# Rebalancing a five-engine pipeline: bias, norm columns, reciprocal roots and a written order for each of two layers

## The chip, the cores and the metric

One core of a Trainium2 chip runs the whole program. The metric is device time in microseconds, median of the runs. Five engines share the work and each runs its own instructions in order: PE (TensorE; PEld is its weight load), DVE (VectorE), ACT (ScalarE), POOL (GpSimd), and SP (SyncE), which here issues nearly all DMAs. They meet only at semaphores.

## The reference, cut to what matters

The input x is 512 x 512 x 64 in float32. Two equal layers follow each other, `x = x + f(gn(x))`:

- `gn` normalizes 32 groups of two channels over the whole image, so it needs sums over all of x before the first point can be worked on. It is an affine step per channel.
- `xn = ln(gn(x))` over the 64 channels of a point.
- `left`, `right` and `gate` are products of `xn` with 64 x 128 weights, `left` and `right` times a sigmoid of a second product, `gate` a sigmoid.
- A band: `out[i, j] = sum over d in -4..4 of left[i + d, i] * right[i + d, j]`, for each of 128 channels.
- `out = ln(out) * gate` over the 128 channels, then `out @ Wo + bo`, added to x.

## The kernel before

**Tiles and steps.** The rows are cut into 9 blocks (`row_blocks`, line 67), and each block's columns into 2 chunks of 16 steps, 288 steps a layer. A step `t` handles a *unit* of 8 columns from each half of the image, on 128 partitions, as a tile `z` of 128 x (8 x 64) numbers (`load`, line 391). The first layer writes `mid_x`, the second reads it and writes the output; the same generator `layer` (line 739) does both, with `stats` true for the first, which also sums up what the second layer's `gn` needs (`sums`, line 727). Between the layers `mid_stats` (line 924) works out that affine step.

**The path of a unit.** POOL scales and moves it by the group norm (`affine`, line 427; in the first steps of a layer DVE does this). DVE takes statistics (`inner_stats`, line 432, mean and variance of two columns by one instruction). POOL subtracts the mean and multiplies by the reciprocal root (`inner_norm`, line 436). PE transposes it (`transposed`, line 442), ACT copies that out (`kept`, line 461) and it goes to DRAM for later use as well. PE forms two products of four columns each (`right`, line 506), ACT the sigmoid, DVE the product into the ring `RO` (`right_end`, line 513).

**The path of a result.** When a chunk of `RO` is full, PE forms the band with the left factors (`mix`, line 567), two PSUM banks at a time, one copied back into `RO` by ACT and one by DVE. DVE takes the statistics (`out_stats`, line 592), ACT normalizes 8 columns, one instruction each (`norm`, line 631), PE transposes (`turned`, line 668), DVE multiplies by the gate (`times_gate`, line 681), PE multiplies by `Wo` (`end`, line 704), and DVE adds that to the x of that place (`ended`, line 718), which SP has fetched again and to which POOL has added the bias of the layer (`biased`, line 698).

**The roots.** Every four steps `solve` (line 598) turns the variances of four units and four results into reciprocal roots: DVE prepares them with small instructions, and `rsqrt` (line 134) does a first guess on DVE and ten dependent instructions of 128 x 64 on POOL; two more follow there for the results.

**Shifted sums.** Before, the first layer's bias has a per-group mean subtracted, so that the sums it collects are of small numbers, and the second layer's bias has it added again (`shifted`, line 282).

**PSUM.** There are eight banks. `one_bank` (line 128) gives single banks, three in the first layer and four in the second; `two_banks` (line 131) gives pairs, of which there are two. The products, the transposed units and (at the start) the left factors take pairs; gates, turned results, last products and bands take single banks.

**What sets the order.** The loop over `t` (lines 806 to 909) issues everything by wrappers (`en`, line 375) that keep each engine's instructions in the order of the program text, so the order in which the parts stand in that loop is the order in every engine's queue. All of these instructions bear the line of the wrapper, L373, in the profile, and are told apart by their tiles. Tables (`look`, `step`, `count`) place statistics, bands and affine steps in the steps. For POOL the order within a step is: mean and root of the unit after next, scale and move, the roots (every fourth step, one after the other), bias, and then, in those steps, scale and move of one more unit.

Of the kernel before, what the change touches and what calls it, by code (L numbers as in the profile page):

```python
# [30 lines left out]
LN_EPS = 1e-6  # L31

# [47 lines left out]
def tile_two_banded_layers(  # L80
# [35 lines left out]
    nc.vector.memset(all_ones, 1.0)  # L116
    ones_row = const.tile([1, P], F32, name="ones_row")
# [16 lines left out]
    def rsqrt(o: bass.AP, v: bass.AP, vec=nc.vector, e=nc.vector):  # L134


        p, n = v.shape
        t, u = (
            sm.tile([P, 3 * NB], F32, tag=f"rsqrt{i}", name="rsqrt", bufs=1)[:p, :n]
            for i in range(2)  # L140
        )
        vec.tensor_scalar(
            o.bitcast(I32), v.bitcast(I32), -0.5, float(0x5F3759DF), ALU.mult, ALU.add
        )
        e.tensor_tensor(t, o, o, ALU.mult)
        e.tensor_tensor(t, t, v, ALU.mult)
        e.tensor_scalar(u, t, -10.0 / 3.0, None, ALU.add)
        e.tensor_tensor(t, t, u, ALU.mult)
        e.tensor_scalar(t, t, 5.0, None, ALU.add)
        e.tensor_tensor(o, o, t, ALU.mult)  # L150
        e.tensor_tensor(t, o, o, ALU.mult)
        e.tensor_tensor(t, t, v, ALU.mult)
        e.tensor_scalar(t, t, -27.0 / 1024.0, 0.5625, ALU.mult, ALU.add)
        e.tensor_tensor(o, o, t, ALU.mult)


    PARTS = (
        ("right", 2 * H), ("left", 2 * H), ("gate", H), ("Wo", D), ("ob", 1), ("add", 2 * D),
# [60 lines left out]
    def solve_layer(i: int, f: dict, r: dict, tmp, half: bass.AP):  # L219
# [36 lines left out]
        add = r["add"].rearrange("p (t c) -> p t c", c=D)  # L256
        nc.vector.tensor_copy(add[:, 0, :], pb[:, :D])
# [24 lines left out]
    def shifted(i: int, r: dict, tmp):  # L282
        add = r["add"].rearrange("p (t c) -> p t c", c=D)
        if i == 0:

            bias = tmp.tile([P, G], F32, name="bias")
            nc.vector.tensor_reduce(
                bias, add[:, 0, :].rearrange("p (g t) -> p g t", t=2), AX.X, ALU.add
            )
            nc.vector.scalar_tensor_tensor(bias, bias, 0.5, total, ALU.mult, ALU.add)  # L290
            spread(shift, bias)
        op = ALU.add if i else ALU.subtract
        nc.vector.tensor_tensor(add[:, 0, :], add[:, 0, :], shift, op)
        nc.vector.tensor_copy(add[:, 1, :], add[:, 0, :])


# [6 lines left out]
    shift = const.tile([P, D], F32, name="shift")  # L303
# [4 lines left out]
    def group_affine(mean: bass.AP, var: bass.AP, pool):  # L308

        ve = pool.tile([P, D], F32, name="g_ve")  # L310
        nc.vector.tensor_scalar(ve, var, GN_EPS, None, ALU.add)
        rsqrt(ga, ve)
        nc.vector.scalar_tensor_tensor(gb, mean, -1.0, ga, ALU.mult, ALU.mult)
# [113 lines left out]
    def affine(u: Unit, engine):  # L427

        engine.tensor_tensor(u.z, u.z, mid(ga, JU), ALU.mult)
        engine.tensor_tensor(u.z, u.z, mid(gb, JU), ALU.add)  # L430
# [5 lines left out]
    def inner_norm(u: Unit):  # L436
        z = u.z.rearrange("p (k t) c -> p k t c", t=2)
        m = u.mean.unsqueeze(3).broadcast_to([P, JU // 2, 2, D])
        en.gpsimd.tensor_tensor(z, z, m, ALU.subtract)
        en.gpsimd.tensor_tensor(u.z, u.z, last(u.rs, D), ALU.mult)  # L440
# [126 lines left out]
    def mix(c: int, A: bass.AP, h0: int) -> list:  # L567
# [6 lines left out]
        ph = [one_bank().rearrange("i (h t j) -> i h t j", h=q, t=2) for s in range(2)]  # L574
# [23 lines left out]
    def solve(w: dict, ins: list, outs: list, sti, sto):  # L598
# [3 lines left out]
        r = sm.tile([P, 3 * NB], F32, tag="rs", name="rs", bufs=3)[:, : ni + no]  # L602
        if ni:
            en.vector.tensor_scalar(
                v[:, :ni].rearrange("p (k t) -> p k t", t=2), sti[:, : ni // 2, 2::3],
                1.0 / D, LN_EPS, ALU.mult, ALU.add,
            )
            for n, u in enumerate(ins):
                u.rs = r[:, n * JU : (n + 1) * JU]
        if no:  # L610

            js = slice(outs[0].m, outs[0].m + no)
            vo = v[:, ni:]
            en.vector.scalar_tensor_tensor(
                vo.rearrange("p (k t) -> p k t", t=2), sto[:, :, 2::3], 1.0 / H,
                w["m2"][:, js].rearrange("p (k t) -> p k t", t=2), ALU.mult, ALU.mult,
            )
            en.vector.tensor_scalar(vo, vo, LN_EPS, None, ALU.add)
            nm = sm.tile([P, NB], F32, tag="nm", name="nm")[:, :no]
            en.vector.tensor_scalar(  # L620
                nm.rearrange("p (k t) -> p k t", t=2), sto[:, :, 1::3], -1.0, None, ALU.mult
            )
        rsqrt(r, v, en.vector, en.gpsimd)
        if no:
            ro = r[:, ni:]
            en.gpsimd.tensor_tensor(ro, ro, w["m"][:, js], ALU.mult)
            en.gpsimd.tensor_tensor(nm, nm, ro, ALU.mult)
            for n, o in enumerate(outs):
                o.rs, o.nm = ro[:, n * JU : (n + 1) * JU], nm[:, n * JU : (n + 1) * JU]

    def norm(o: Out, lo: int, hi: int):
        if lo == 0:
            o.on = onp.tile([P, JU, H], F32, tag="on", name="on")
        for j in range(lo, hi):
            en.scalar.activation(
                o.on[:, j, :].rearrange("p (h t) -> p h t", t=2), RO[:, :, o.c + j, :],
                AF.Identity, bias=o.nm[:, j : j + 1], scale=o.rs[:, j : j + 1],
            )
# [59 lines left out]
    def biased(o: Out, w: dict, stats: bool):  # L698
        n = S + o.blk.m
        f = o.xr[:n, :, 1 : 1 + 2 * D]  # L700
        add = fewer if stats and o.blk.m < S - WIN else w["add"]
        en.gpsimd.tensor_tensor(f, f, mid(add[:n], JU // 2), ALU.add)

    def end(o: Out, w: dict):
        m = o.blk.m
# [33 lines left out]
    def layer(src: bass.AP, dst: bass.AP, w: dict, stats: bool, then=None):  # L739
# [59 lines left out]
        A, sti, sto, then_affine = {}, {}, None, []  # L799
        for t in range(min(loads), last_t + 3):  # L800
# [21 lines left out]

            mixing, mixed = mixes.get(t, []), []
# [10 lines left out]

# [3 lines left out]
            for v in looking[0:3]:  # L838
                out_stats(*v)
            for u in inputs(t + 2):  # L840
                inner_norm(u)
            if t in units:
                right(units[t], 0, w)
            if t in units:
                right_gate(units[t], 0)
            if t in outs:
                gates(outs[t], w)
            if t in units:
                right(units[t], JQ, w)
            for u in affines.pop(t, []):  # L850
                affine(u, en.vector if u.at < NU + 4 else en.gpsimd)
            if t % 4 == 0 and t > NU:
                then_affine = affines.pop(t + 1, [])
            for v in looking[3:5]:
                out_stats(*v)
            for v in looking[5:]:
                out_stats(*v)
            for v in todo:
                inner_stats(*v)
            if t % 4 == 0:  # L860
                st, us = sti.pop((t + 4) // 4, (None, []))
                so, os = sto or (None, [])
                sto = None
                if us or os:
                    solve(w, us, os, st, so)
            if t in outs:
                gated(outs[t])
            if t in units:
                right_end(units[t], 0)
            if t in outs:  # L870
                biased(outs[t], w, stats)
            if t in outs:
                turned(outs[t], w)
            if t in units:
                right_gate(units[t], JQ)
            for u in inputs(t + 1):
                transposed(u)
            if t in outs:
                times_gate(outs[t], w)
            for u in then_affine:  # L880
                affine(u, en.gpsimd)
            then_affine = []
            if t - 1 in outs:
                end(outs[t - 1], w)
            if t in units:
                right_end(units[t], JQ)
            if len(mixing) > 0:
                c, h0 = mixing[0]
                mixed.append(mix(c, A[c, h0 // HA], h0))
            if t + 1 in outs:  # L890
                norm(outs[t + 1], 0, 4)
            for u in inputs(t + 1):
                kept(u)
            if stats and t - 2 in outs:
                sums(outs[t - 2], t - 2 == first_t, t - 2 == last_t)
            if len(mixing) > 0:
                en.scalar.copy(*mixed[0][0])
            if t - 1 in outs:
                ended(dst, outs[t - 1])
            if t + 1 in outs:  # L900
                norm(outs[t + 1], 4, 8)
            if len(mixing) > 1:
                c, h0 = mixing[1]
                mixed.append(mix(c, A[c, h0 // HA], h0))
            if len(mixing) > 0:
                en.vector.tensor_copy(*mixed[0][1])
            if len(mixing) > 1:
                en.scalar.copy(*mixed[1][0])
            if len(mixing) > 1:
                en.vector.tensor_copy(*mixed[1][1])  # L910
# [136 lines left out]
```

## Time and profile before

| what | value |
|---|---|
| median of 3 runs | 4814.17 us (4813.22 to 4815.75) |
| the profiled execution | 4808.51 us, its span 4806.5 us |
| busy share of the span | PE 79%, DVE 82%, ACT 77%, POOL 79% |
| granted TensorE clock, mean | 0.948 |
| DMA | 983.63 MB moved, 205 GB/s |
| first layer's steady steps | from about 500 to 2400 us |
| second layer's steady steps | from about 2800 to 4600 us |

The shares are taken over the whole span, in which the statistics of the input (the first 250 us) and the change of layers (2400 to 2800 us) use the engines little. What bounds the two long stretches is read from those stretches alone. A row of a group of instructions gives: engine, operation, what it writes and reads, shapes, how many, then busy time, mean duration in ns, and the idle time in front of them with what ended it. A row of the timeline gives start, length, engine, operation and tiles. An instruction's length includes the time in which it has started and doesn't get at its data.

### The profile page before, as it was taken

Reading aid. Unit: us, or ns where it says so; the run is one execution under the profiler, and the core shown is the slowest. Engines: PE = TensorE matmul, PEld = TensorE weight load, DVE = VectorE, ACT = ScalarE, POOL = GpSimd, SP = SyncE. Lnnn points to the kernel's source line nnn. Section 1 sums busy time; section 2 is a strip of 40 time slices with the busy share of each in tenths; the row PEclk is TensorE's granted clock in tenths of the full one; section 3 lists DMA queues with packets and bytes.
Section 4 is the critical chain, followed back from the end, with each engine's and each line's share of the span. In section 5 each row is a group of like instructions: output and inputs, shape, how many; then the busy total and the mean of one; then the engine's idle time right before and its main releaser. Section 6 shows DMA issues by size and latency. Waiting matters only on the chain. (4 is left out here: it accounts for less than half of the span.)

```text
span 4806.5 us, 193543 instructions
## 1 busy us (share of the span) xinstructions
PE 3796.6 (79%) x76306; PEld 3293.0 (69%) x76306; DVE 3929.9 (82%) x9635; ACT 3708.4 (77%) x8732; POOL 3817.1 (79%) x4739
## 2 busy tenths in 40 slices
PE   1025799989999999999985478888888888888888
PEld 0024688878888887888854467777777777777775
DVE  6954788888888888888867478888888888888887
ACT  0013689888888898989883268888888888888899
POOL 0035999999999999999734589999999999999964
PEclk9997999999999999999997689999999999999999
DMA  7859677777777777777763967777777777777876
GB/s 299 336 178 108 172 212 213 215 210 215 211 209 210 211 214 212 214 212 215 199 170 100 105 168 212 216 214 209 217 213 215 213 213 218 210 216 211 222 200 179
DMA packets 1437651, 983.63 MB, mean 205 GB/s; under 512 B 167202, under 2 KB 1284424, under 8 KB 1432392
## 3 DMA queue, kind: packets, MB, share of 16 engines
q1 hardware_dynamic: 1432064, 969.75, 73.6%
q8 instruction: 604, 9.90, 0.9%
q14 instruction: 303, 2.48, 0.2%
q10 hardware_dynamic: 4680, 1.50, 0.1%
HBM read 658.42 MB, written 312.46 MB: 202 GB/s over the span
## 5 line engine op out<-in xcount | busy, mean ns | idle before, releaser
L373 ACT ACTIVATE on<-RO,nm,rs 128x128 f32<-128x128 f32 x4608 | 1927.7, 496 | 15.3 <-PE bank L373 9.9
L373 PEld LDWEIGHTS banks<-pack,zT 64*128 64x128 f32 x18576 | 1251.3, 195 | 549.5 <-ACT zT L373 288.9
L373 PE MATMUL banks<-pack,zT 64*128 64x128 f32 x18576 | 1365.6, 289 | 272.8 <-ACT zT L373 222.6
L373 DVE TENSOR_TENSOR RO<-banks,sg 128x512 f32<-128x512 f32 (+1 forms) x1188 | 795.3, 673 | 228.3 <-POOL sg L373 116.2
L373 DVE SCALAR_TENSOR_TENSOR ZH<-bank,pack,gate 128x448 f32<-128x448 f32 (+1 forms) x1152 | 741.6, 685 | 173.3 <-PE bank L373 97.3
L373 ACT ACTIVATE sg<-banks 128x512 f32<-128x512 f32 (+1 forms) x1188 | 698.0, 589 | 188.6 <-PE banks L373 188.2
L373 DVE BATCH_NORM_STATS2 sto<-RO 128x6 f32<-128x256 f32 x2304 | 800.8, 411 | 3.7
L373 POOL TENSOR_TENSOR z<-z,gb 128x512 f32<-128x512 f32 x536 | 684.8, 1278 | 42.0
L373 PE MATMUL bank<-RO,A 64*64 64x128 f32 x18432 | 706.0, 292 | 3.9 <-ACT RO L373 2.4
L373 PE MATMUL bank<-pack,ZH 128*64 128x64 f32 x18432 | 694.6, 231 | 5.0 <-ACT gate L373 4.1
L373 POOL TENSOR_TENSOR z<-z,ga 128x512 f32<-128x512 f32 x536 | 685.6, 1279 | 3.2 <-DMA z<-mid_x 1.9
L373 POOL TENSOR_TENSOR z<-z,rs 128x512 f32<-128x512 f32 x586 | 619.3, 1057 | 46.0
L373 DVE COPY RO<-bank 128x512 f32<-128x512 f32 x576 | 398.4, 692 | 310.6 <-PE bank L373 307.3
L373 PEld LDWEIGHTS bank<-pack,ZH 128*64 128x64 f32 x18432 | 612.6, 143 | 47.3 <-ACT gate L373 8.5
L373 POOL TENSOR_TENSOR z<-z,sti 128x512 f32<-128x512 f32 x586 | 627.9, 1072 | 0.0
L373 PEld LDWEIGHTS bank<-RO,A 64*64 64x64 f32 x18432 | 582.0, 142 | 43.0 <-ACT RO L373 4.1
L373 ACT ACTIVATE gate<-bank 128x448 f32<-128x448 f32 (+1 forms) x1152 | 565.8, 545 | 34.5 <-PE bank L373 32.0
L373 ACT ACTIVATE zT<-banks 128x512 f32<-128x512 f32 (+1 forms) x1084 | 463.5, 481 | 139.6 <-PE banks L373 128.9
L373 PE MATMUL bank<-zg,pack 64*128 64x448 f32 (+1 forms) x2304 | 564.3, 556 | 4.6 <-DMA zg<-later 4.6
L373 ACT COPY RO<-bank 128x512 f32<-128x512 f32 x576 | 333.2, 579 | 282.3 <-PE bank L373 282.1
L373 PE MATMUL banks<-ident,z 64*128 64x64 f32 x4336 | 254.1, 233 | 359.2 <-DVE RO L373 336.9
L373 DVE BATCH_NORM_STATS2 sti<-z 128x6 f32<-128x128 f32 x2344 | 500.5, 280 | 15.2 <-POOL z L373 14.2
(144 smaller groups left out, 3908.6 us busy)
## 6 DMA issues: line engine op xcount, KB each, us to landing
later<-zT SPq DMA_DIRECT2D x576, 256.0 KB
A<-left_of SPq DMA_DIRECT2D x1152, 128.0 KB
zg<-later SPq DMA_DIRECT2D x576, 256.0 KB
z<-in_x_dram SPq DMA_DIRECT2D x576, 128.0 KB
z<-mid_x SPq DMA_DIRECT2D x576, 128.0 KB
gn_x<-in_x_dram SPq DMA_DIRECT2D x16, 4096.0 KB
XR<-in_x_dram SPq DMA_DIRECT2D x448, 112.0 KB
mid_x<-XR SPq DMA_DIRECT2D x448, 112.0 KB
```

The lines of the kernel that those rows point to most:

```text
L373: return lambda *a, **k: tc.keep_in_program_order(f(*a, **k))
```

## The change

1. **Small forms.** In `solve`, DVE's single-source instructions (`tensor_scalar`) become instructions with two tensors as sources; the epsilon comes from a constant column spread over the width, and a negation is written as `x * 0 - x`. The first guess in `rsqrt` stays as it is.
2. **Norm columns.** Of the 8 columns of a result, ACT normalizes 7 and DVE one (`NV`), by an instruction that reads `RO` and a spread column.
3. **Inner columns.** In the first layer 2 of a unit's 8 columns are centred and scaled by DVE, one instruction a column (`ZV`), and POOL's two instructions cover the other 6; in the second layer nothing moves. The first 17 units are left as they were.
4. **Chains.** `rsqrt` returns its ten POOL instructions as a list, and the loop issues them two at a time between other work; scale and move, and mean and root, are no longer next to each other.
5. **Bias.** The first layer adds both layers' biases (`both`), so that what it stores already holds the second layer's; the second layer issues no bias instruction. `mid_stats` takes that addition out of the sums again, by some small instructions. `shifted` goes.
6. **PSUM.** In the first layer the two banks of a band come as a pair (`APART`), in the second as single banks, as before.
7. **Order.** The loop over the parts of a step follows a list, one for each layer.

```diff
+APART = (False, True)
+ZV = (2, 0)
+NV = (1, 1)
+FIRST = [
+    ("out stats", 2), "centre", "scale", "gates", ("out stats", 3), "inner stats", "bias",
+    "gated", ("project", 0), ("out stats", 99), ("project", 4), "inner columns", "rescale",
+    "turn", "solve", ("sigmoid", 0), ("sigmoid", 4), "last product", ("norm", (0, 4)),
+    "scale next", "move", "move next", ("roots", 2), "sums", ("right", 0), ("roots", 2),
+    ("right", 4), "transpose", "times gate", "keep", ("band", 0), ("band", 1),
+    "norm columns", ("copy a", 0), "end", ("roots", 2), ("copy a", 1), ("copy b", 0),
+    ("roots", 2), ("norm", (4, 8)), ("copy b", 1), ("roots", 99),
+]
+SECOND = [
+    "gates", "scale", "move", ("project", 0), "inner stats", ("project", 4),
+    ("out stats", 2), "centre", ("sigmoid", 0), ("out stats", 3), ("out stats", 99),
+    ("right", 0), "rescale", "inner columns", "gated", "solve", "scale next",
+    ("sigmoid", 4), ("roots", 2), "turn", "last product", "transpose", "times gate",
+    ("band", 0), ("roots", 2), ("norm", (0, 4)), ("roots", 2), "keep", "end", ("right", 4),
+    ("band", 1), ("copy a", 0), "norm columns", ("copy b", 0), ("copy a", 1), ("roots", 2),
+    ("norm", (4, 8)), ("roots", 99), "move next", ("copy b", 1),
+]
...
-    def inner_norm(u: Unit):
-        z = u.z.rearrange("p (k t) c -> p k t c", t=2)
-        m = u.mean.unsqueeze(3).broadcast_to([P, JU // 2, 2, D])
-        en.gpsimd.tensor_tensor(z, z, m, ALU.subtract)
-        en.gpsimd.tensor_tensor(u.z, u.z, last(u.rs, D), ALU.mult)
+    def centred(u: Unit, n: int):
+        m = last(u.mean.rearrange("p k t -> p (k t)")[:, n:], D)
+        en.gpsimd.tensor_tensor(u.z[:, n:], u.z[:, n:], m, ALU.subtract)
+
+    def rescaled(u: Unit, n: int):
+        en.gpsimd.tensor_tensor(u.z[:, n:], u.z[:, n:], last(u.rs[:, n:], D), ALU.mult)
+
+    def inner_columns(u: Unit, n: int):
+        for j in range(n):
+            en.vector.scalar_tensor_tensor(
+                u.z[:, j], u.z[:, j], u.mean[:, j // 2, j % 2 : j % 2 + 1],
+                u.rs[:, j : j + 1].broadcast_to([P, D]), ALU.subtract, ALU.mult,
+            )
...
-        ph = [one_bank().rearrange("i (h t j) -> i h t j", h=q, t=2) for s in range(2)]
+        if APART[0 if stats else 1]:
+            pb = [one_bank() for s in range(2)]
+        else:
+            two = two_banks()
+            pb = [two[:, s * 512 : (s + 1) * 512] for s in range(2)]
...
-            en.vector.tensor_scalar(
-                v[:, :ni].rearrange("p (k t) -> p k t", t=2), sti[:, : ni // 2, 2::3],
-                1.0 / D, LN_EPS, ALU.mult, ALU.add,
+            en.vector.scalar_tensor_tensor(
+                pairs(v[:, :ni]), sti[:, : ni // 2, 2::3], 1.0 / D, eps(ni),
+                ALU.mult, ALU.add,
             )
...
-    def norm(o: Out, lo: int, hi: int):
+    def norm(o: Out, lo: int, hi: int, vector: bool):
...
+            if vector:
+                nm = nm.unsqueeze(2).broadcast_to([P, H // 2, 2])
+                en.vector.scalar_tensor_tensor(to, of, rs, nm, ALU.mult, ALU.add)
+            else:
+                en.scalar.activation(to, of, AF.Identity, bias=nm, scale=rs)
...
-    def biased(o: Out, w: dict, stats: bool):
+    def biased(o: Out, w: dict):
...
-        add = fewer if stats and o.blk.m < S - WIN else w["add"]
+        add = fewer if o.blk.m < S - WIN else both
```

## The prediction

> **What bounds the kernel now.** First the busy time by engine over a long stretch in the middle of each layer, to see whether one engine is full.
>
> ```profile
> 600.00:2200.00 1600.00, 1463.40 (x31066) 1292.29 (x31066) 1372.42 (x3382) 1430.93 (x3332) 1469.33 (x1770) 0.98 0.76 212
> 2800.00:4400.00 1600.00, 1342.77 (x27460) 1178.72 (x27460) 1412.85 (x3396) 1387.89 (x3315) 1480.65 (x1791) 0.95 0.76 211
> ```
>
> After the length the columns are PE, PEld, DVE, ACT and POOL busy, granted clock, DMA share, GB/s. POOL leads in both layers with 92 to 93%, DVE has 86 and 88%. To turn shares into a step I count norm instructions, eight to a step, in the groups of 800 to 2000 us (the first layer):
>
> ```profile
> L373 ACT ACTIVATE on<-RO,nm,rs 128x128 f32<-128x128 f32 x1325 | 555.9, 492 | 1.1 <-ACT sg L373 1.1
> L373 POOL TENSOR_TENSOR z<-z,ga 128x512 f32<-128x512 f32 x168 | 214.9, 1279 | 0.0
> L373 POOL TENSOR_TENSOR z<-z,gb 128x512 f32<-128x512 f32 x168 | 214.8, 1278 | 13.2
> L373 POOL TENSOR_TENSOR z<-z,sti 128x512 f32<-128x512 f32 x166 | 175.3, 1056 | 0.0
> L373 POOL TENSOR_TENSOR z<-z,rs 128x512 f32<-128x512 f32 x165 | 172.1, 1043 | 12.9
> L373 POOL TENSOR_TENSOR XR<-XR,fewer 120x512 f32<-120x512 f32 x166 | 197.3, 1189 | 0.3 <-DMA XR<-in_x_dram 0.2
> ```
>
> 1325/8 = 165.6 steps in 1200 us are 7.25 us a step. The same count in the second layer (1562 norms from 3000 to 4400 us) gives 195.25 steps and 7.17 us. Busy per step is then, first layer: POOL 6.65, PE 6.63, ACT 6.48, DVE 6.21; second: POOL 6.64, DVE 6.33, ACT 6.22, PE 6.02. The rest of POOL's step, about 0.6 us, is idle time in front of its own dependent instructions (the last field of its rows, 98 us in that stretch, 38 of them before the first instruction of the reciprocal roots). So POOL has no time left over; it sets the step.
>
> **What two sources cost on DVE.** The change gives DVE instructions with two tensors in SBUF, beside a busy POOL. The steady stretch has no large one, but the start of each layer has: there DVE scales and moves the units. DVE, then POOL, from 345 us:
>
> ```profile
> 345.93 0.85 DVE L373 TENSOR_TENSOR z<-z,ga 128x512 f32<-128x512 f32 x1
> 346.81 1.41 DVE L373 TENSOR_TENSOR z<-z,gb 128x512 f32<-128x512 f32 x1
> ```
> ```profile
> 346.31 1.37 POOL L373 TENSOR_TENSOR z<-z,rs 128x512 f32<-128x512 f32 x1
> 347.64 1.50 POOL L373 TENSOR_TENSOR z<-z,sti 128x512 f32<-128x512 f32 x1
> ```
>
> and at 303 us on DVE:
>
> ```profile
> 303.44 0.69 DVE L373 TENSOR_TENSOR z<-z,gb 128x512 f32<-128x512 f32 x1
> 304.05 1.54 DVE L373 TENSOR_TENSOR z<-z,ga 128x512 f32<-128x512 f32 x1
> ```
>
> Alone the DVE instruction takes 0.69 us (303.44 in the last fence). At 346.81 it takes 1.41, of which 0.72 is waiting, up to about 0.15 us before POOL's row ends at 347.68. POOL's own rows grow from 1.05 to 1.37 and 1.50. So the two exclude each other for whole instructions. The pair at 304.05 shows the order: two units, independent of each other, and yet POOL gets its turn between them (its row of 303.47 lasts 1.58), so that the second DVE instruction waits for a whole POOL instruction.
>
> **The change part by part.** The profiled execution took 4808.5 us (span 4806.5); the median of the three runs is 4814.2, so 5.7 is added at the end.
>
> *POOL.* In the second layer the bias leaves (1.19 a step: 128x512 group at 1189 to 1190 ns): 6.64 becomes 5.45. In the first, centring and rescaling keep 6 of 8 columns: (1.06 + 1.04)/4 = 0.53 less, 6.12. The interleaved roots and the split of scale and move take away most of the 0.6 us of gaps. POOL no longer bounds: 6.1 to 6.2 and 5.5. What is late next is DVE or PE.
>
> *ACT.* One norm column of eight goes: 0.42 us a step (1.69 for four in a row), leaving 6.06 and 5.80. In steady state it is covered. In the two tails, where a step takes 4.55 us and ACT is 4.24 of it (3.24 for eight norms, 1.00 for the gates), it is not covered: 30 steps a layer x 0.41 x 2 = 24, taken as -20 because the chain's other links remain.
>
> *DVE, own time.* No row shows the new form on 128x64 or 128x128. Between the two-source rows at hand, 186 ns for 128x32 (var<-sto,pack) and 691 for 128x512, a straight line gives 220 and 287 ns; neighbours overlap by some 60 ns (four statistics of 411 ns take 1.40), so 0.15 and 0.22 us each. First layer: 2 x 0.15 + 0.22 = 0.52 a step; second 0.22. So DVE without further waits would be 6.73 and 6.55.
>
> *DVE, waits.* From below, nothing (a form that takes another way to memory); from above, a whole POOL instruction each, 1.28 us. I take the rule of the fences, which are the nearest rows. POOL's five large instructions of the first layer would be 0.79, 0.79, 1.28, 1.28, 1.19; the mean remainder met by chance is the sum of squares over twice the sum, 0.56, less the 0.15 at the end, 0.42; POOL is at work some 85% of the time: 0.36 us for the norm column and for the first inner column. The second inner column follows directly and meets a whole new POOL instruction: mean 1.07 less 0.1, at 80%: 0.75. Together 1.47 us a step in the first layer, 0.36 in the second. Behind the waiting instruction on DVE stand the products `right`, the gate product, the residual sum and the band copies, and PE waits for those to get its PSUM banks back: nothing hides it once DVE is full.
>
> The Trainium skill ("SBUF — State Buffer", section "Who interferes with whom") goes further than these rows: any VectorE instruction with two SBUF inputs contends with a GpSimd instruction that reads SBUF, which takes in the scalar forms used here; by it the sum stays as it is, and without it it is rival A. Its "GPSIMD Engine Reference" (section "Engine selection") speaks for the change: elementwise work belongs on VectorE, twice as fast; by it 0.53 us of POOL would cost DVE 0.30 and the result would again be rival A, but the fenced row of 1.41 us beside POOL is no faster than POOL's 1.28.
>
> *The solve.* Its single-source instructions wait for POOL too (var<-sti has a mean of 501 ns in the first layer's stretch and 665 in the second's, where 0.17 is the least). With two sources they meet the same exclusion; I cost the new forms at 0. If they did not wait, they would give back 0.15 and 0.31 us a step; if each of five met a POOL instruction, that is up to 5 x 1.1/4 = 1.4 us lost, less what it costs now. Against that end: POOL, ahead of DVE, will often be waiting for just this solve.
>
> *Sum.* A full engine still idles a little behind others; I allow 2%. First layer: 1.02 x (6.73 + 1.47) = 8.36, 1.12 more than 7.25, over the 271 steps that have inner columns: +303. Second: 1.02 x (6.55 + 0.36) = 7.05, 0.12 less, x 288: -35. Tails -20. The added dozen small instructions between the layers and the dropped ones of the setup are about 1 us each way. 4808.5 + 303 - 35 - 20 + 5.7 = **5062 us**.
>
> SP's queue keeps its transfers; loads go out in the same place. The new orders move instructions only within a step; I give them no gain, as I see none to read from a row.
>
> **Rivals.** With a factor f on all these waits the sum is -264 + 512 f (first layer 271 x (1.50 f - 0.38), second 288 x (0.37 f - 0.49), tails -20): zero at f = 0.52.
>
> *A, faster:* the scalar form on DVE doesn't queue behind POOL, or POOL mostly stands idle when it comes. At f = 0 the steps are 6.87 and 6.68: 4814 - 264 = 4550; with the solve's waits gone too, some 4430, since PE holds the first layer at 6.63. It decides below a mean wait of about 0.25 us for each such instruction. For it: POOL will have idle time, unlike now, and the fenced rows are of another opcode. Against it: exclusion shows in every pair where both are at work.
>
> *B, slower still:* the bands of the first layer move from the single PSUM banks to the two double ones, which then have four tenants a step instead of three. Now PE waits there already (for DVE's RO 91 us from 800 to 2200). If the late DVE holds both pairs so that PE is late in turn and DVE then waits for PE, I add 0.6 us a step: +163, 5225.
>
> *C, nothing comes of it:* f near 0.5, the second layer's gain pays for the first's loss: 4805 to 4824.
>
> **Chances.** Forecast (4824 to 5200) 0.54, B and beyond 0.17, A 0.26, C 0.03. So faster by over 0.2% 0.26, within 0.2% (about what a measurement of this kernel can tell from no change) 0.03, slower 0.71. The range goes from 4620 (f = 0.14) to 5270 (f = 1.4): about 0.12 lies below it and 0.08 above. The likeliest case's own range is 4824 to 5200.
>
> **What will show it.** DVE's share in the first layer over 95%, POOL's near 75%; the inner-column rows at a mean of 0.5 to 0.9 us instead of 0.22, the norm column at 0.65; POOL's rows of 384 elements longer than 0.79; POOL waiting for the solve longer than now. Rows of 0.22 and 0.29 us beside a busy POOL would make the prediction wrong, and so would a first layer that stays near 7.2 us a step.

## The result and the profile after

The changed kernel takes 5034.4 us (median of 4 runs, 5030.58 to 5046.85), the kernel before 4814.87 beside it: ratio 1.0461 [1.0442, 1.0479]. The forecast was 5062, slower. The profiled execution took 5035.45 us, its span 5033.7, 227.2 more than before.

Where that came from is read from the gate products on DVE, two to a step, in both traces. First product of the first layer: 531.3 us instead of 541.2 (-9.9; over all the runs of this document it lies between 521.9 and 546.9, so this is not read). From first to last product of the first layer: 2279.5 instead of 2015.2 (+264.3). From there to the second layer's first: +1.2. Second layer: 1941.1 instead of 1969.4 (-28.3). What follows: -0.1. As a mean over steps 40 to 250 the first layer goes from 7.23 to 8.30 us a step, the second from 7.14 to 7.07. The whole loss lies in the first layer. Its granted clock is lower too (0.94 instead of 0.98 from 800 to 2200 us), but that is not what costs: executions of the changed kernel with 0.906, 0.934, 0.909 and 0.935 over the span took 5035.45, 5033.36, 5046.85 and 5030.58 us, and the four of e6 below, at 0.925 to 0.950, were fastest at the lowest clock.

Busy time of each engine in a stretch of each layer, changed kernel, columns as in the prediction:

```profile
600.00:2200.00 1600.00, 1337.16 (x26860) 1174.95 (x26860) 1543.41 (x3504) 1178.29 (x2687) 1183.65 (x1536) 0.93 0.66 184
3200.00:4600.00 1400.00, 1242.43 (x24647) 1079.95 (x24647) 1281.95 (x3226) 1188.88 (x2782) 1096.39 (x1392) 0.97 0.78 216
```

In the first layer DVE is busy 96% of the time and POOL 74%: "over 95%" and "near 75%" were forecast. In the second, DVE has 92% and POOL 78%: no engine is full there. The groups of 800 to 2000 us, changed kernel:

```profile
L389 DVE SCALAR_TENSOR_TENSOR z<-z,sti,rs 128x64 f32<-128x64 f32 x290 | 204.9, 746 | 0.0
...
L389 POOL TENSOR_TENSOR XR<-XR,fewer 120x512 f32<-120x512 f32 x145 | 173.7, 1198 | 254.0 <-DMA XR<-in_x_dram 186.8 <-PE banks L389 16.2 <-PE bank L389 13.9
...
L389 POOL TENSOR_TENSOR z<-z,rs 128x384 f32<-128x384 f32 x145 | 121.7, 839 | 0.0
L389 POOL TENSOR_TENSOR z<-z,sti 128x384 f32<-128x384 f32 x144 | 121.0, 840 | 0.0
...
L389 DVE SCALAR_TENSOR_TENSOR on<-RO,rs,nm 128x128 f32<-128x128 f32 x145 | 74.8, 516 | 0.0
...
L389 DVE SCALAR_TENSOR_TENSOR var<-sti,ln_eps 128x32 f32<-128x32 f32 x36 | 28.6, 794 | 0.0
L389 DVE SCALAR_TENSOR_TENSOR var<-sto,pack 128x32 f32<-128x32 f32 x36 | 24.4, 679 | 0.0
```

An inner column takes 746 ns, the norm column 516; POOL's rows of 384 elements take 839 and 840 instead of the 0.79 us that their size would give. The directions were forecast, and the sizes too, but for the norm column (0.65 us). One sign did not come: POOL should have waited longer for the solve, and in the first layer it waits 0.75 us for each instead of 0.83 (31.7 us in 42 solves, 39.8 in 48, 800 to 2200 us); in the second it does, 1.08 instead of 0.50 (3200 to 4600 us). Two things were not forecast. POOL now stands idle for 254 us of 1200 in front of its *bias* instruction, 187 of them for the fetch of `XR`; before, these were 0.3. And the small instructions of the solve wait: the product `var<-sto,pack` took 188 ns before and takes 679.

How an inner column waits, and what POOL waits for, in the timeline of the changed kernel:

```profile
1406.08 0.84 POOL L389 TENSOR_TENSOR z<-z,sti 128x384 f32<-128x384 f32 x1
1406.20 2.04 DVE L389 SCALAR_TENSOR_TENSOR z<-z,sti,rs 128x64 f32<-128x64 f32 x2
...
1406.51 1.03 SPq L389 DMA_DIRECT2D XR<-in_x_dram  x2
...
1406.88 1.28 POOL L389 TENSOR_TENSOR z<-z,ga 128x512 f32<-128x512 f32 x1
...
1410.49 1.20 POOL L389 TENSOR_TENSOR XR<-XR,fewer 120x512 f32<-120x512 f32 x1 [2.33 <-DMA XR<-in_x_dram]
1410.55 1.29 DVE L389 SCALAR_TENSOR_TENSOR on<-RO,rs,nm 128x128 f32<-128x128 f32 x1
...
1416.44 0.46 DVE L389 SCALAR_TENSOR_TENSOR z<-z,sti,rs 128x64 f32<-128x64 f32 x2
```

The pair at 1406.20 takes 2.04 us: its first instruction waits for POOL's of 1406.08, its second until nearly the end of the one of 1406.88 (POOL ends at 1408.16, the pair at 1408.24). The norm column, which starts 0.06 us after a POOL instruction of 1.20, takes 1.29. The pair at 1416.44 meets an idle POOL and takes 0.46. That is the exclusion of the prediction: here DVE and POOL meet not only at semaphores. But POOL had been idle for 2.33 us before 1410.49, and SP had issued that fetch only at 1406.51.

### The profile page after: what moved, and what is told of

Its sections match the earlier page's. It is cut to its first block, busy times and chain, and to the rows that moved or that the text cites. A ratio compares the mean times of both kernels' runs of the same rounds, so it can differ in the third digit from the quotient of the medians.

```text
span 5033.7 us, 192903 instructions
## 1 busy us (share of the span) xinstructions
PE 3947.1 (78%) x76306; PEld 3407.3 (68%) x76306; DVE 4455.6 (89%) x10755; ACT 3532.9 (70%) x8156; POOL 3371.0 (67%) x4451
## 5 line engine op out<-in xcount | busy, mean ns | idle before, releaser
L389 ACT ACTIVATE on<-RO,nm,rs 128x128 f32<-128x128 f32 x4032 | 1705.1, 504 | 23.5 <-POOL nm L389 9.0
L389 PEld LDWEIGHTS banks<-pack,zT 64*128 64x128 f32 x18576 | 1324.7, 203 | 408.0 <-ACT zT L389 232.5
L389 PE MATMUL bank<-zg,pack 64*128 64x448 f32 (+1 forms) x2304 | 741.4, 633 | 170.6 <-DMA zg<-later 111.2
L389 PE MATMUL bank<-pack,ZH 128*64 128x64 f32 x18432 | 667.3, 226 | 3.3 <-ACT gate L389 0.5
L389 POOL TENSOR_TENSOR z<-z,rs 128x512 f32<-128x512 f32 (+1 forms) x586 | 565.0, 965 | 23.3
L389 POOL TENSOR_TENSOR z<-z,sti 128x512 f32<-128x512 f32 (+1 forms) x586 | 568.3, 971 | 0.0
L389 POOL TENSOR_TENSOR XR<-XR,fewer 120x512 f32<-120x512 f32 x224 | 268.5, 1198 | 388.7 <-DMA XR<-in_x_dram 290.1
L389 PE MATMUL bank<-ident,on 64*128 64x64 f32 x9216 | 468.0, 227 | 32.6 <-ACT gate L389 25.7
L389 PEld LDWEIGHTS bank<-ident,on 64*128 64x128 f32 x9216 | 437.7, 141 | 79.2 <-ACT gate L389 33.2
L389 PEld LDWEIGHTS bank<-zg,pack 64*128 64x128 f32 x2304 | 254.3, 197 | 291.4 <-issue 86.2
```

The lines of the kernel that those rows point to most:

```text
L389: return lambda *a, **k: tc.keep_in_program_order(f(*a, **k))
```

## The experiments

The theory was: DVE is full because its two-source instructions wait for POOL (**port waits**). The rivals that the runs weigh: the new order of the first layer, the pair of PSUM banks, the interleaved roots. Steps are means over steps 40 to 250; the DVE share is that of 800 to 2200 us; ratios stand against the kernel before on the same chip. The short names are explained below. Each step time is from one traced execution, on one of several chips, on which the kernel before took medians of 4810 to 4839 us. First layers of the same program differ by 0.03 us a step (e10 and e12), second layers of the same program by up to 0.09 (after, e1, e2, e6 to e9: 7.04 to 7.13). Smaller differences are not read.

| kernel | first layer, us a step | its DVE share | second layer, us a step | ratio to before |
|---|---|---|---|---|
| before | 7.23 | 86% | 7.14 | 1 |
| after | 8.30 | 97% | 7.07 | 1.0461 [1.0442, 1.0479] |
| e1, no inner columns | 8.03 | 90% | 7.13 | 1.0307 [1.0279, 1.0335] |
| e2, inner columns' second source in PSUM | 8.05 | 93% | 7.08 | 1.0305 [1.0286, 1.0323] |
| e3, no columns | 8.05 | 84% | 7.10 | 1.0353 [1.0325, 1.0381] |
| e4, bias alone | 7.19 | 86% | 6.98 | 0.9864 [0.984, 0.9888] |
| e5, e3 with bias last | 7.40 | 87% | 7.14 | 1.0012 [0.9998, 1.0027] |
| e6, after with bias last | 7.73 | 99% | 7.09 | 1.0161 [1.0138, 1.0183] |
| e7, old order with columns | 8.33 | 91% | 7.11 | 1.0465 [1.0432, 1.0497] |
| e8, after with single banks | 8.67 | 92% | 7.04 | 1.0654 [1.0633, 1.0676] |
| e9, e7 with second sources in PSUM | 7.51 | 88% | 7.08 | 1.0023 [1.0014, 1.0033] |
| e10, e4 with the two-source solve | 7.18 | 86% | 6.98 | 0.9848 [0.9831, 0.9864] |
| e11, e4 with interleaved roots | 7.38 | 83% | 7.01 | 0.9963 [0.9948, 0.9978] |
| e12, e10 with a norm column in the second layer | 7.21 | 86% | 6.99 | 0.9871 [0.9854, 0.9887] |

### Taking back the columns, and the bias alone

**e1** puts the inner columns back to POOL:

```diff
-ZV = (2, 0)
+ZV = (0, 0)
```

> The changed kernel with the inner columns given back to GpSimd in the first layer, all else kept (order, norm column, band pair). Port theory (a VectorE instruction with two SBUF sources queues behind GpSimd): VectorE loses 2 x 0.70 us a step of the first layer, which goes from 8.30 to about 7.0 us, 271 steps, so about 4680 us (4640 to 4760). Rival 'work' (VectorE just has more to do, 0.15 us a column): first layer at 8.0, about 4950. Rival 'order' (the new order or the band's pair of banks costs the time): first layer stays above 8, 4950 or more.

**e2** leaves them on DVE, in the same places, but their second source is a block of ones in PSUM. It leaves the reciprocal root out of these columns.

```diff
-                u.rs[:, j : j + 1].broadcast_to([P, D]), ALU.subtract, ALU.mult,
+                ones_ps, ALU.subtract, ALU.mult,
...
+    ones_ps = acc_bank[:, 256 : 256 + D]
+    nc.vector.memset(ones_ps, 1.0)
```

> The changed kernel, but the two inner columns read their second source from a constant tile of ones in PSUM instead of the roots in SBUF; this leaves the multiplication by the root out of those two columns. Count, size and place of the instructions stay. Port theory: their mean goes from 746 to about 220 ns, the first layer to about 7.0 us a step, about 4670 us (4620 to 4760). Rivals 'work' and 'order': nothing changes, 5034 us.

**e3** takes back the norm columns too:

```diff
-ZV = (2, 0)
-NV = (1, 1)
+ZV = (0, 0)
+NV = (0, 0)
```

> The changed kernel without inner columns and without norm columns on VectorE in both layers; order, forms, bias and the band's pair stay. Port theory: another 0.45 us off VectorE and 0.42 us onto ScalarE a step; the first layer near 6.9, the second from 7.07 to about 6.75, in all about 4570 us (4500 to 4680). Rival 'order': the first layer stays above 8 us, the second at 7.05, 4950 or more.

**e4** keeps only part 5 of the change, the bias stored by the first layer; order, small forms, chains and banks are those of before.

```diff
-APART = (False, True)
+APART = (True, True)
-ZV = (2, 0)
-NV = (1, 1)
+ZV = (0, 0)
+NV = (0, 0)
-ORDERS = (FIRST, SECOND)
+ORIG = [
+    ("out stats", 3), "centre", "rescale", ("project", 0), ("sigmoid", 0), "gates",
+    ("project", 4), "scale", "move", ("out stats", 2), ("out stats", 99), "inner stats", "solve",
+    ("roots", 99), "gated", ("right", 0), "bias", "turn", ("sigmoid", 4), "transpose",
+    "times gate", "scale next", "move next", "last product", ("right", 4), ("band", 0),
+    ("norm", (0, 4)), "keep", "sums", ("copy a", 0), "end", ("norm", (4, 8)), "norm columns",
+    ("band", 1), ("copy b", 0), ("copy a", 1), ("copy b", 1),
+]
+SECOND_ORIG = [x for x in ORIG if x not in ("bias", "sums")]
+ORDERS = (ORIG, SECOND_ORIG)
...
-            en.vector.scalar_tensor_tensor(
-                pairs(v[:, :ni]), sti[:, : ni // 2, 2::3], 1.0 / D, eps(ni),
-                ALU.mult, ALU.add,
-            )
+            en.vector.tensor_scalar(
+                pairs(v[:, :ni]), sti[:, : ni // 2, 2::3], 1.0 / D, LN_EPS, ALU.mult, ALU.add
+            )
...
```

> The kernel before with one part of the change alone: the first layer stores the second's bias, and GpSimd has no bias instruction in the second layer. Order, small forms, band banks, all columns as before. Theory: the first layer stays at 7.23; in the second GpSimd falls to about 6.0 us a step with its gaps and VectorE, 6.33 us busy, bounds: 6.5 to 6.7 us, 288 steps, about 4640 us (4600 to 4700). Rival (something else held the second layer as well, a transfer or PSUM): 7.0 us or more there, 4770 us or more.

The row of the inner columns in e2, from the groups of 800 to 2200 us (in the changed kernel the same stretch gives 743 ns):

```profile
L389 DVE SCALAR_TENSOR_TENSOR z<-z,sti,acc 128x64 f32<-128x64 f32 x346 | 78.7, 269 | 0.0
```

Same operation, size and place, and the waiting is gone: 269 ns. That these columns no longer depend on the root is not the reason: in the changed kernel DVE stands idle for 0.2 us in all in front of them. So it is the second source *in SBUF* that waits for POOL. The Trainium skill ("SBUF — State Buffer", section "Who interferes with whom") says so of VectorE instructions with two SBUF inputs beside a GpSimd instruction that reads SBUF; this pair of rows agrees.

But the time fell short of the theory. Without any waiting of the inner columns the first layer still takes 8.05 us a step, and without columns at all (e3) the same 8.05. The busy times of e3, 800 to 2200 us:

```profile
800.00:2200.00 1400.00, 1221.22 (x24394) 1057.26 (x24391) 1172.76 (x2662) 1106.77 (x2601) 1140.48 (x1394) 0.93 0.69 190
```

PE 87%, DVE 84%, ACT 79%, POOL 81%: nothing is full, and still a step takes 0.82 us more than before. So the columns' port waits cannot be the only cause. (Port waits as such are not gone: the five small rows of the solve take 0.95 us a step in e3, 0.38 in the kernel before. But DVE has idle time.) Some of the longest sums in the waits of the same stretch of e3 (us in total, times, the longest):

```profile
PEld banks L389 <- POOL rsqrt L389: 124.6, 33, 5.4
POOL XR L389 <- DMA XR<-in_x_dram: 117.2, 46, 6.0
...
ACT on L389 <- POOL nm L389: 51.8, 11, 5.6
```

One such place in the timeline of e3, on POOL:

```profile
1412.03 1.29 POOL L389 TENSOR_TENSOR z<-z,ga 128x512 f32<-128x512 f32 x1
1419.33 1.18 POOL L389 TENSOR_TENSOR XR<-XR,fewer 120x512 f32<-120x512 f32 x1 [6.01 <-DMA XR<-in_x_dram]
...
1429.49 0.25 POOL L389 TENSOR_TENSOR nm<-nm,rs 128x32 f32<-128x32 f32 x1
```

The list `FIRST` has "bias" in seventh place, `ORIG` (the order of before) in the middle of the step. SP issues the fetch of `XR` in its own order, behind the stores of the step before: `later<-zT`, which waits for ACT, and `mid_x<-XR`, which waits for DVE (230.7 and 12.5 us of SP's waits in e3, 236.7 and 95.5 in the changed kernel, 100.0 and 10.6 before). Here SP issued it at 1414.13. POOL reaches the bias long before the data, stands for 6.01 us, and behind the bias in its in-order queue stand rescaling, moving and the ten roots. The roots' last product `nm` comes at 1429.49, and ACT's norm columns, at 1429.78, have waited for it for 5.50 us. From the end of the issue of a result's fetch to its bias the median over results 100 to 260 is 8.4 us in the kernel before, 3.5 in the changed kernel and 4.0 in e3; the least is 2.0 to 2.2 in all three. This would be a second cause, the **early bias**; the next experiments separate it.

e4 beats the kernel before: 0.9864.

### Two causes apart

**e5** is e3 with "bias" moved to the end of the first layer's list; **e6** is the changed kernel with the same one move.

```diff
-    ("out stats", 2), "centre", "scale", "gates", ("out stats", 3), "inner stats", "bias",
+    ("out stats", 2), "centre", "scale", "gates", ("out stats", 3), "inner stats",
...
-    ("roots", 2), ("norm", (4, 8)), ("copy b", 1), ("roots", 99),
+    ("roots", 2), ("norm", (4, 8)), ("copy b", 1), ("roots", 99), "bias",
```

> As e3_both_back (no columns on VectorE), and in the first layer's list the bias moves from the front of GpSimd's work in a step to its end. New theory ('early bias'): in the changed order GpSimd meets the bias about half a step earlier than before, in front of the transfer that it adds to, and everything behind it on GpSimd (mean, roots) comes late; then the first layer falls from 8.05 to about 7.2 us a step or less, 240 us off e3. Port theory: nothing here, 8.05 stays, since no columns are left on VectorE. Rival 'pair' (the band's pair of banks): 8.05 stays as well.

> The changed kernel with only the bias moved to the end of GpSimd's work in a step of the first layer; columns, pair and the rest of the order stay. Port theory: VectorE's own time with its waits is 8.0 us a step and the first layer stays at 8.2 to 8.3. 'Early bias' alone: 7.2 to 7.5. Both as causes that hide each other: 8.2 here and 7.2 in e5.

**e7** has all columns, but the first layer's order and banks of before (`ORIG` with "inner columns" behind the second "project"):

```diff
-APART = (False, True)
+APART = (True, True)
-ORDERS = (FIRST, SECOND)
+ORDERS = (ORIG, SECOND)
```

> The changed kernel with the old order and the old single banks in the first layer alone; inner and norm columns stay on VectorE, the second layer is as changed. Port theory: VectorE's rows keep their waits and the first layer is at 8.0 or more, against 7.2 before. 'Early bias' or 'pair' alone: 7.2 or a little less, since GpSimd has 0.5 us less to do.

**e8** is the changed kernel with single banks for the first layer's bands (rival B):

```diff
-APART = (False, True)
+APART = (True, True)
```

> The changed kernel with the band's two banks taken singly in the first layer, as before. 'Pair': the first layer falls from 8.30 to 7.5 or less. Port theory and 'early bias': 8.2 to 8.3 stays.

In e5 the bias finds its data. Its row, 800 to 2200 us (in e3 the idle time is 211.2, in the changed kernel 291.6):

```profile
L389 POOL TENSOR_TENSOR XR<-XR,fewer 120x512 f32<-120x512 f32 x188 | 223.4, 1188 | 24.3 <-DMA XR<-in_x_dram 15.8 <-PE banks L389 7.0 <-DVE sti L389 1.2
```

and the step falls from 8.05 to 7.40; from fetch to bias there are now 8.2 us. With the columns (e6) it falls from 8.30 to 7.73, and now DVE really is what is full:

```profile
800.00:2200.00 1400.00, 1214.24 (x25348) 1055.58 (x25346) 1383.56 (x3301) 1108.36 (x2532) 1122.15 (x1447) 0.98 0.72 198
```

That is 1383.56 of 1400 us. Not all that the early bias costs is a wait for data: from the changed kernel to e6 DVE's busy time falls from 8.02 to 7.64 us a step, and the solve's five rows from 0.60 to 0.24. So with the early bias DVE's small instructions also met more of POOL's large ones.

e7, with the order of before, keeps the whole loss: 8.33. So the columns are enough by themselves. In e7 DVE has 91%, and what it delays is seen in the waits:

```profile
POOL rsqrt L398 <- DVE rs L398: 286.5, 42, 9.3
PEld banks L398 <- DVE RO L398: 273.2, 162, 3.5
PE banks L398 <- DVE RO L398: 251.0, 161, 3.3
```

POOL waits 6.8 us for each solve (39.8 us in 48 times in the kernel before), because DVE comes late to it, and PE waits for DVE's products.

e8 is worse than the changed kernel, 8.67 against 8.30; ACT waits 180.5 us for a single bank of the bands. So in this order the pair of banks helps by 0.37 us a step: rival B had the wrong sign.

The first layer's step, order against columns (all have the two-source solve; the first row has single banks, the others the pair):

| first layer's order | no columns | columns | the columns cost |
|---|---|---|---|
| of before | 7.18 (e10) | 8.33 (e7) | 1.14 |
| new, bias last | 7.40 (e5) | 7.73 (e6) | 0.33 |
| new | 8.05 (e3) | 8.30 (after) | 0.26 |

Read down, the new order without its early bias costs 0.22 without columns and *gains* 0.59 with them; the early bias then costs 0.64 or 0.57. Read across, the columns cost 1.14 in the old order and little in the new.

### Port waits in the old order, and the parts that remain

**e9** is e7 with the second source of the inner and norm columns taken from PSUM, in the first layer. It leaves the root out of the inner columns and the mean term out of the norm column.

```diff
-                u.rs[:, j : j + 1].broadcast_to([P, D]), ALU.subtract, ALU.mult,
+                ones_ps[:, :D], ALU.subtract, ALU.mult,
...
+                if first_layer[0]:
+                    nm = ones_ps.rearrange("p (h t) -> p h t", t=2)
...
```

> As e7 (old order, single banks, columns on VectorE in the first layer), but there both column forms read their second source from a constant tile of ones in PSUM; this leaves the root out of the inner columns and the mean term out of the norm column. Port theory: the rows go from 674 and 561 to about 270 and 300 ns, VectorE loses 1.1 us a step, and the first layer falls from 8.33 to about 7.1 to 7.3, 300 us off e7. Rival (the extra work or the coupling of the columns, not the port): 8.0 or more stays.

**e10** is e4 with the two-source forms in the solve:

```diff
-            en.vector.tensor_scalar(
-                pairs(v[:, :ni]), sti[:, : ni // 2, 2::3], 1.0 / D, LN_EPS, ALU.mult, ALU.add
-            )
+            en.vector.scalar_tensor_tensor(
+                pairs(v[:, :ni]), sti[:, : ni // 2, 2::3], 1.0 / D, eps(ni),
+                ALU.mult, ALU.add,
+            )
...
```

> e4_bias_alone plus the two-source forms in the solve, nothing else. The prediction's cost of nothing: within 0.4% of e4's ratio to the kernel before (0.9864), each layer within 0.05 us a step. If the forms don't wait for GpSimd they give back up to 0.15 us a step in the first layer and 0.1 in the second, 70 us.

**e11** is e4 with the roots issued two at a time between POOL's other work; "rescale" and "move" stand later for that:

```diff
-    ("out stats", 3), "centre", "rescale", ("project", 0), ("sigmoid", 0), "gates",
-    ("project", 4), "scale", "move", ("out stats", 2), ("out stats", 99), "inner stats", "solve",
-    ("roots", 99), "gated", ("right", 0), "bias", "turn", ("sigmoid", 4), "transpose",
-    "times gate", "scale next", "move next", "last product", ("right", 4), ("band", 0),
-    ("norm", (0, 4)), "keep", "sums", ("copy a", 0), "end", ("norm", (4, 8)), "norm columns",
-    ("band", 1), ("copy b", 0), ("copy a", 1), ("copy b", 1),
+    ("out stats", 3), "centre", ("project", 0), ("sigmoid", 0), "gates", ("project", 4), "scale",
+    "rescale", ("out stats", 2), ("out stats", 99), "inner stats", "solve", "move", "gated",
+    ("right", 0), ("roots", 2), "bias", ("roots", 2), "turn", ("sigmoid", 4), "transpose",
+    "times gate", "scale next", ("roots", 2), "move next", ("roots", 99), "last product",
+    ("right", 4), ("band", 0), ("norm", (0, 4)), "keep", "sums", ("copy a", 0), "end",
+    ("norm", (4, 8)), ("band", 1), ("copy b", 0), ("copy a", 1), ("copy b", 1),
```

> e4_bias_alone plus chains interleaved on GpSimd in both layers: scale and move, mean and root apart, the ten root instructions two at a time between other work; bias no earlier than before, VectorE's, ScalarE's and TensorE's order as before. If GpSimd's gaps of 0.6 us a step are what the first layer has to give: 7.0 us there, 60 us off e4. Rival: the roots end later, the norms on ScalarE wait for them, and the step stays at 7.2 or grows.

The rows of the columns in e7, then in e9, 800 to 2200 us:

```profile
L398 DVE SCALAR_TENSOR_TENSOR z<-z,sti,rs 128x64 f32<-128x64 f32 x336 | 213.4, 674 | 0.0
...
L398 DVE SCALAR_TENSOR_TENSOR on<-RO,rs,nm 128x128 f32<-128x128 f32 x167 | 93.8, 561 | 0.0
```
```profile
L398 DVE SCALAR_TENSOR_TENSOR z<-z,sti,acc 128x64 f32<-128x64 f32 x374 | 85.2, 269 | 0.0
...
L398 DVE SCALAR_TENSOR_TENSOR on<-RO,rs,acc 128x128 f32<-128x128 f32 x186 | 63.9, 344 | 117.0 <-PE acc L398 117.0
```

The columns now take 269 and 344 ns (674 and 561 in e7), and the step falls from 8.33 to 7.51. So some 0.8 of the 1.14 that the columns cost in the old order is waiting for the second SBUF source: 0.82 by these steps, 0.78 by the medians (5062.38 and 4850.26 us, over 271 steps). In e7 DVE was never idle in front of these rows, so the dependency that e9 drops is not what it gains. It may be more than 0.8, since the experiment adds a wait: the ones share a tile with the sums in PSUM, so that the norm column waits for PE, 117 us in 186 steps, 0.63 a step. How much faster e9 would be without it was not measured.

e10 against e4: 7.18 and 7.19, 6.98 and 6.98. The two-source forms of the solve cost nothing where the order is that of before. The row of the epsilon instruction in e10:

```profile
L398 DVE SCALAR_TENSOR_TENSOR var<-sti,ln_eps 128x32 f32<-128x32 f32 x49 | 25.9, 528 | 0.0
```

The single-source form in the same place in e4 takes 446 ns: both wait.

e11 costs 0.19 us a step in the first layer (7.38 against 7.19). In 800 to 2200 us ACT waits 33.3 us in 22 places for `nm`, the roots' last product, a wait that e4 does not have, and POOL waits 79.2 us for the solve instead of 44.2. This is the rival's direction: roots that leave POOL no gaps, but end later.

### A norm column in the second layer

**e12** is e10 with the norm column on DVE in the second layer alone, where ACT is at 90% (e4, 3200 to 4600 us: 1264.64 of 1400).

```diff
-NV = (0, 0)
+NV = (0, 1)
```

> e10_bias_and_forms plus the norm column on VectorE in the second layer alone, old order. There GpSimd works 77% of the time. Port theory: the row has a mean near 0.55 us where it is 0.29 alone, VectorE goes from 6.03 to about 6.5 us a step, ScalarE from 6.32 to 5.9. Since neither is then full, the second layer (6.98) could move either way, 6.8 to 7.1, 4710 to 4800 us. If the column cost only its own 0.22 us it would be 6.7 to 6.8.

The row of e12, 3200 to 4600 us:

```profile
L398 DVE SCALAR_TENSOR_TENSOR on<-RO,rs,nm 128x128 f32<-128x128 f32 x201 | 132.1, 657 | 0.0
```

DVE goes to 1308.64 of 1400 us (93%), ACT falls to 1217.90 (87%), and the step is 6.99 instead of 6.98. Nothing is gained; the ratio to before, 0.9871 [0.9854, 0.9887], is not told apart from e10's 0.9848 [0.9831, 0.9864]. The fastest versions are e10, e12 and e4, all with the bias stored by the first layer and the order of before.

## Why the prediction was right, and what it had not seen

**Right in number, sign and bound.** 5062 us was forecast and 5034.4 came; first layer 8.36 forecast and 8.30 measured, second 7.05 and 7.07. In the first layer DVE is the full engine and POOL falls to 74%.

**Port waits: right as a mechanism, shown by itself.** An inner column takes 746 ns beside POOL and 269 with its second source in PSUM; e7 has the loss of the first layer (8.33) with the order of before, and e9 takes some 0.8 of it back. DVE's own time with its waits was forecast at 8.20 us a step; the changed kernel shows 8.02 (96.6% of 8.30). That this is so near is in part luck. Measured against their forms with a PSUM source, the two inner columns and the norm column wait for 1.12 us a step (2 x (743 - 269) + 520 - 344 ns), not 1.47. Against that, their own time is 0.16 more than the straight line gave (269 and 344 ns instead of 220 and 287), and the solve takes 0.22 more, not 0.

**The step that failed** is the one on the order: "The new orders move instructions only within a step; I give them no gain, as I see none to read from a row." Zero is near the net effect (old order 8.33, new 8.30, both with columns), but by luck: two terms of some 0.6 us cancel. The early bias costs 0.57 (e6 to after); the rest of the new order and the pair of banks, taken together, gain 0.59 for a kernel with the columns (e7 to e6; how much of this is the pair's was not tried in that order). The clue was in the trace of before, where the fetch of a result and its bias are 9.2 us apart:

```profile
1401.06 0.99 SPq L373 DMA_DIRECT2D XR<-in_x_dram  x2
```
```profile
1410.29 1.18 POOL L373 TENSOR_TENSOR XR<-XR,fewer 120x512 f32<-120x512 f32 x1
```

A bias that is moved towards the front of the step, while SP's queue stays as it is, can come before its data; in the changed kernel POOL waits for that fetch in 66 of 168 steps (800 to 2200 us). The prediction said that SP's queue keeps its transfers and asked no further.

**Two causes that hide each other.** Taking back only the columns, or a part of them, gives 0.25 to 0.27 us a step (e1, e2, e3), because the early bias keeps the step at 8.05; taking back only the early bias gives 0.57 (e6); both together give 0.90 (e5). The expectations of the port theory for e1 to e3, which put the whole loss down to these columns, were wrong.

**Smaller terms.** The solve was costed at 0: in the old order that is right (e10 against e4), in the changed kernel its five instructions cost 0.22 us a step more than before in the first layer (0.60 against 0.38, the sum of their means over four steps), where several meet a POOL instruction each, and 0.17 less in the second (0.38 against 0.55, 3200 to 4600 us). Without the inner columns' waits the solve waits more, not less (0.99, 1.01 and 0.95 us a step in e1, e2 and e3). The norm column was forecast at 0.65 us and takes 516 ns; in e6, where POOL is idle for 65.4 us in front of the bias and not for 291.6, it takes 649. The second inner column's wait was put at 0.75, but its own factors, (1.07 - 0.1) x 0.8, give 0.78, some 8 us in all. Rival B had the wrong sign (e8).

**The second layer: right number, partly for another reason.** DVE was forecast to be full there; it has 92%. Leaving out the bias frees POOL of 1.19 us a step, but brings only 0.17 (e4: 7.14 to 6.98), and the changed second layer gives about 0.1 of that back (6.98 to 7.01 in e4 and e10 to e12, 7.04 to 7.13 with the changed second layer). e3, whose second layer has the new order without the norm column, is at 7.10, so the column is not what gives it back. Some of POOL's and PE's longer waits in the changed second layer, 3200 to 4600 us, are for transfers:

```profile
POOL z L389 <- DMA z<-mid_x: 153.7, 64, 5.2
...
PE bank L389 <- DMA zg<-later: 80.6, 41, 3.8
```

**What stays open.** All versions of the second layer lie between 6.98 and 7.14 with no engine over 94%; what holds it there was not settled. Of the 0.22 us that the new order without its early bias still costs without columns (e5 against e10), the interleaved roots are a fitting candidate (0.19 in e11, in the other order), but that was not tried in the new order. There are two others in the same rows: the solve takes 0.69 us a step in e5 and 0.40 in e10, and POOL waits 0.27 us a step for the fetch of the units (51.7 us for `z<-in_x_dram` in 800 to 2200 us), which e10 does not.

## What to carry to other kernels

Before an elementwise instruction is moved from GpSimd to VectorE, count its sources in SBUF: beside a busy GpSimd each instruction with two of them is to be costed with a wait of up to one GpSimd instruction, and consecutive ones with one each. When an instruction is moved forward in an in-order queue, look up when its transfer is issued and behind what; one wait at the front delays everything behind it. When taking back a suspected cause gives back too little, a second cause may hide it: take back both, and each alone, and put the four times in a table.

## What the runs showed of the hardware that was not expected

- A second source in PSUM takes away the waiting entirely: 128x64 in 269 ns against 743 (e2 against the changed kernel), 128x128 in 344 against 561 (e9 against e7). The longest of these in PSUM takes 292 and 353 ns; in SBUF the shortest takes 256 and 340, the longest 1351 and 1381.
- The small single-source forms of VectorE wait beside GpSimd like the two-source ones (446 ns in e4 and 528 in e10, in the same place of the first layer; 166 and 179 ns in their second layers, where GpSimd stands waiting for just this solve).
- Ten short dependent GpSimd instructions lose some 0.07 to 0.09 us between each other (in e3 one of 0.32 us starts at 1425.56 and the next at 1425.96), but filling these gaps with other work made the kernel slower (e11, 0.9963 of the kernel before, against 0.9864 for e4).
